# A four-layer graph network on one core: layer 3's first pair placed in layer 2, roots as powers on GpSimd, finer steps in the chains, and another split of the squares

## The chip, the cores and the metric

The kernel runs on one core of one Trainium2 chip. The metric is the device time of one execution in microseconds (us), over three runs of the kernel before. A core has a matrix engine (TensorE, PE; its weight loads are listed as PEld), a vector engine (VectorE, DVE), a scalar engine (ScalarE, ACT), a general engine (GpSimd, POOL) and an engine that here only issues transfers (SyncE, SP). Each engine works through its own instructions in their fixed order and waits on semaphores for the others.

## The reference, cut to what matters

`x` is 3327 x 64, `adj` is a dense 3327 x 3327 matrix with few nonzero values. Four layers follow each other; each takes a layer norm of `x` with a ReLU, a function of it and `adj`, and adds the result to `x`.

```python
h = maximum(layernorm(x), 0); x = x + ggc(ggc(h, adj), adj)  # layer 0, two gated steps
h = maximum(layernorm(x), 0); x = x + hyperbolic(h, adj)     # layer 1: adj @ h, norms, tanh, artanh
h = maximum(layernorm(x), 0); x = x + ranked(h, adj)         # layer 2:
#   mask = adj != 0; rank = cumsum(mask, 1); w = mask * 0.5 ** (k - pos); w @ (h @ weight) + bias
h = maximum(layernorm(x), 0)                                 # layer 3:
adj_att = sigmoid(left + right.T) * adj                      # per pair of nodes
x_local = logmap(h[:, None, :], h[None, :, :])               # per pair of nodes
s = einsum('ij,ijd->id', adj_att, x_local)
x = x + proj(expmap(h, s))                                   # per node: norms, tanh, quotients
```

## The kernel before

The nodes are padded to 26 blocks of 128 and stand on the free axis of the transposed matrix. They are cut into two target groups: group 0 with 12 blocks (1536 columns) and group 1, called `gf`, with 14 (1792 columns); `gs_` is group 0. A tile of `adj` is one source block by one target group: 768 or 896 KB. Every layer reads such tiles through one stream. `uses_of_tiles` (L125) lists all uses in order; `Stream` (L137) keeps tiles in numbered slots and, at each `done`, loads those up to 6 or 10 uses ahead that find a slot. `limit` (L155) says how many slots each layer has: 16 in layers 0 and 1, 7 in layer 2, 4 in layer 3. SP issues all loads, at L262.

Small chains of work for the nodes (norms, quotients, transposes) are Python generators. `Weave` (L81) advances each of them by one step at every `tick`, between the steps of the large loops, and a `yield 2` skips a tick. That is how the order on each engine comes about: what a generator issues before its next `yield` stands as one piece in the engines' queues.

Layer 1's result goes through `support` (L711), once per group, which also prepares layer 2's operands. `norm` (L443) and `layernorm_relu` (L450) take their square roots on ACT, followed by a reciprocal on DVE. ACT holds one set of function tables at a time; a root needs another set than Tanh or Gelu.

Layer 2 (L948 to L1046) goes over 52 tiles, 26 for group 1, then 26 for group 0. For tile n DVE makes the mask (L961) two tiles ahead, PE counts ranks with two triangular products per half (L975, L983) into a pair of PSUM banks, ACT turns counts to weights by a Relu (L991), and two tiles later PE multiplies the weights by three bfloat16 parts of the operands (L1009). After group 1's last tile its result is evicted, and `nodes3(gf)` (L819) makes what layer 3 needs of these nodes, in ticks between group 0's tiles: layer norm, `x2`, `q`, the scaled nodes `xd`, `pn` and its inverse `rpn`, transposed copies `xs` and `xw`, packed rows `rows_i`, `rows_j`, and `leftb`. `nodes3(gs_)` follows inside layer 3 and uses one PSUM bank, `turn["banks"] = (1,)`.

Layer 3 (L1140 to L1349) goes over 26 pairs of source blocks: 13 for the targets of group 1 and 13 for group 0; pairs 0 to 6 have sources in `gf`. For a pair, `distances(n, k)` runs PE (L1159, L1171), a Gelu over the result (L1179) and a Tanh (L1186) on ACT, for k = 0 and 1. `weights` (L1208) multiplies the Tanh by two adj tiles on DVE (L1214). `squares` (L1198) squares the Gelu's two halves: `a` on ACT (L1202), `b` in part on ACT (L1203) and the rest on DVE (L1204), cut by `split`. `products3` (L1217) multiplies both on DVE (L1223), and `gather` and `gather_p` (L1235, L1252) sum over sources on PE. The loop is skewed by two:

```python
for n in range(-2, len(pairs)):
    if n >= 0: products3(n); weave.tick()
    if 0 <= n + 1 < len(pairs): distances(n + 1, 1); weave.tick()
    if n >= 0: gather(n)
    if 0 <= n + 1 < len(pairs): weights(n + 1); weave.tick(); squares(n + 1); weave.tick()
    if n + 2 < len(pairs): begin(n + 2); distances(n + 2, 0); weave.tick()
    if n >= 0: gather_p(n)
    weave.tick()
```

After pair 12 group 1 is evicted, and `collected` with `finish` (L1053) computes its output in ticks beside pairs 13 and later; after pair 25 the same runs for group 0 with nothing beside it, and ends the kernel. A general branch after L1353 is for other inputs and is not taken.

Of the kernel before, what the change touches and what calls it, by code (L numbers as in the profile page):

```python
# [18 lines left out]
D = 64  # L19
# [24 lines left out]
SLOTS3, SLOTS2, SLOTS01 = 4, 7, 16  # L44
# [80 lines left out]
def uses_of_tiles():  # L125

    last_first = [2 * c + h for h in (1, 0) for c in reversed(range(HB))]
    layer2 = [(g, k) for g in (1, 0) for k in last_first]
    layer3 = [(g, k) for g in (1, 0) for k in F_SRC + S_SRC]
    starts, uses = [], []  # L130
    for u in (FIRST + SECOND + THIRD, LAYER1, layer2, layer3):
        starts.append(len(uses))
        uses += u
    return uses, starts[1:]


class Stream:  # L137
# [17 lines left out]
    def limit(self, t):  # L155
        layer = sum(t >= s for s in self.starts)
        return (SLOTS01, SLOTS01, SLOTS2, SLOTS3)[layer]

    def next_use(self, s, t):
# [4 lines left out]
        for u in range(t, len(self.uses)):  # L164
            if self.uses[u] == key:
                return u if s < self.limit(u) else len(self.uses)
        return len(self.uses)

    def ahead(self):
        most = AHEAD[self.now >= len(FIRST + SECOND)]  # L170
        for u in range(self.now, min(self.now + most, len(self.uses))):
            key = self.uses[u]
            if any(k == key and s < self.limit(u) for s, (k, _) in self.slots.items()):
                continue
            wanted = set(self.uses[self.now : u + 1])
            able = [
                s for s, (k, _) in self.slots.items() if s < self.limit(u) and k not in wanted
# [8 lines left out]
    def tile(self, u):  # L186
# [4 lines left out]
            if k == self.uses[u] and s < self.limit(u)  # L191
# [13 lines left out]
def gnn_kernel(ctx: ExitStack, tc: tile.TileContext, t, out):  # L205
# [13 lines left out]

    p0 = ctx.enter_context(left("p0"))  # L220
# [36 lines left out]
    def load_tile(s, key):  # L257
        g, k = key
        pool = slots_a if s < SLOTS3 else slots_b if s < SLOTS2 else slots_c
        a = pool.tile([P, WIDE], F32, name="adj", tag=f"adj{s}")  # L260
# [18 lines left out]
    V.memset(eps, LN_EPS)  # L279

# [162 lines left out]
    def norm(g, src, name):  # L443
        r = yield from sumsq(g, src, name)
        S.activation(r, r, AF.Sqrt)
# [4 lines left out]
    def layernorm_relu(g, dst):  # L450
# [8 lines left out]
        S.activation(var, var, AF.Sqrt, bias=eps, scale=1.0 / D)  # L459
        yield  # L460
        rstd = recip(g, var, "ln_rstd")
# [249 lines left out]
    def support(g, m_t):  # L711
# [5 lines left out]
        mn = yield from norm(g, mx, "n1")  # L717
# [28 lines left out]
        yield from layernorm_relu(g, h_n)  # L746
# [72 lines left out]
    def nodes3(g, m_t):  # L819
# [4 lines left out]
        yield from layernorm_relu(g, hv)  # L824
# [13 lines left out]
        S.activation(pn[:, sl], xv, AF.Sqrt)  # L838
# [12 lines left out]
        V.tensor_scalar(pn[:, sl], pn[:, sl], MIN_NORM, None, op0=OP.max)  # L851
        V.reciprocal(rpn[:, sl], pn[:, sl])
        V.tensor_mul(uq, uq, rpn[:, sl])
# [94 lines left out]
    with ExitStack() as c2:  # L948
        mk = c2.enter_context(right("l2"))
        WB = 7  # L950
        LAG = 2
        work = stream.uses[stream.starts[1] : stream.starts[2]]
# [3 lines left out]
        def mask(n):  # L956
            if n < len(work):
                a = stream.tile(stream.starts[1] + n)
                g = GROUPS[work[n][0]]
                masks[n] = mk.tile([P, WIDE], BF16, name="mask", tag="mask", bufs=4)  # L960
                V.tensor_scalar(masks[n][:, : 2 * g.w], a, 0.0, None, op0=OP.not_equal)  # L961

        def count(n, h):
# [3 lines left out]
            if h == 0:  # L967
                ws[n] = mk.tile([P, WIDE], U16, name="w", tag="w", bufs=WB)
# [62 lines left out]

        mask(0)
        mask(1)
        for n in range(len(work)):
            mask(n + 2)
# [4 lines left out]
            todo += [(n, 0), (n, 1)]  # L1040
            flush(n, 4 if len(todo) > 2 * LAG + 2 else 2)
            weave.tick()
        flush(len(work) + LAG, len(todo))
        m_s = evicted(gs_, acc2[0], b_l2)
        weave.until(need["nodes"])
# [7 lines left out]
    def finish(g):  # L1053
# [25 lines left out]
        yield  # L1079
        V.tensor_reduce(ss, w2, axis=AX.X, op=OP.add)  # L1080
        yield
# [4 lines left out]
        al = mul("f_al", fac, B)  # L1086
        be = small(g, "f_be")
        V.scalar_tensor_tensor(be, hs, 2.0, sd, op0=OP.mult, op1=OP.subtract)
        V.tensor_mul(be, be, fac)
        su = mul_add("f_su", al, ss, be, hs)  # L1090
        yield
        hu = mul_add("f_hu", al, hs, be, x2g)
# [4 lines left out]
        V.tensor_scalar(hl, Bp, MIN_NORM, None, op0=OP.max)  # L1097
        V.reciprocal(hl, hl)
        tau = mul("f_tau", pn[:, sl], hl)
        S.activation(tau, tau, AF.Tanh)  # L1100
# [5 lines left out]
        V.scalar_tensor_tensor(xy, hu, 2.0, tau, op0=OP.mult, op1=OP.mult)  # L1106
        V.tensor_scalar(xy, xy, 1.0, None, op0=OP.add)
# [3 lines left out]
        V.tensor_add(rden, rden, xy)  # L1111
# [511 lines left out]
```

## Time and profile before

| | us |
|---|---|
| three runs | 780.57, 780.72, 782.84 |
| median | 780.72 |
| profiled execution | 781.49 |
| its span, first to last instruction | 779.7 |
| PE busy | 670.8 |
| DVE busy | 452.7 |
| ACT busy | 419.2 |
| POOL busy | 4.8 |
| layers 0 and 1, until about | 308 |
| layer 2, until about | 469 |
| layer 3, until about | 751.6 (last gather starts) |
| last finish and output | to 779.7 |

Busy time counts an engine's instructions, not its waits. Matmuls are pipelined, so a full PE row is not PE at its peak. The span lies 1.8 us below the profiled execution's own time, and that execution 0.8 above the median. The mean granted TensorE clock was 0.958 of full speed. 229 tile loads took a median of 6.6 us (768 KB) and 7.5 us (896 KB) from issue to landing.

### The profile page before, as it was taken

What the parts mean: (1) busy time and instruction counts of PE and PEld (TensorE: products, weight loads), DVE (VectorE), ACT (ScalarE), POOL (GpSimd) and SP (SyncE); (2) the same over time, 40 slices, a digit from 0 to 9 for tenths busy, and PEclk for the clock granted to TensorE, in tenths of its full rate; (3) what the DMA queues carried; (4) which work ended last, traced back from release to release, by engine and by line L of the source; (5) the groups of instructions that cost most, each with busy time, mean ns of one, the idle gap of its engine ahead of it and who ended that gap; (6) DMA issues with size and microseconds to landing.
All of it is one profiled execution on the core that took longest, in us unless ns stands there. A gap on an engine that the chain in (4) does not pass through costs nothing. (4 is left out here: it accounts for less than half of the span.)

```text
span 779.7 us, 10293 instructions
## 1 busy us (share of the span) xinstructions
PE 670.8 (86%) x4141; PEld 292.3 (37%) x4141; DVE 452.7 (58%) x749; ACT 419.2 (54%) x489; POOL 4.8 (1%) x11
## 2 busy tenths in 40 slices
PE   4988998898879987799989995788999987799970
PEld 2423442343323333344445452333434433344430
DVE  4403002205776034853366425787999978999976
ACT  3203001203553023666666768777999966799941
POOL 0000000000000001000000000000000000000000
PEclk9999999999999999999999998699999998999995
DMA  8999893699949999989867842224555542265400
GB/s 348 413 407 418 325 366 157 212 391 417 415 176 421 417 414 417 417 323 340 279 224 243 298 152 95 95 95 156 192 191 205 172 165 82 104 211 193 164 1 24
DMA packets 34327, 197.56 MB, mean 253 GB/s; under 512 B 3808, under 2 KB 4448, under 8 KB 34272
## 3 DMA queue, kind: packets, MB, share of 16 engines
q1 hardware_dynamic: 34272, 196.84, 66.6%
q8 instruction: 34, 0.56, 0.3%
q14 instruction: 21, 0.17, 0.1%
HBM read 195.97 MB, written 0.85 MB: 252 GB/s over the span
## 5 line engine op out<-in xcount | busy, mean ns | idle before, releaser
L487 PE MATMUL bank<-adj,m_a 128*64 128x384 f32 (+1 forms) x832 | 159.5, 526 | 10.8 <-DMA adj<-in_adj 10.8
L991 ACT ACTIVATE w<-pair,ebias 128x896 uint16<-128x896 f32 (+1 forms) x104 | 94.4, 949 | 37.0 <-PE pair L983 36.5
L1159 PE MATMUL pair<-xw,xs 64*128 64x384 f32 x208 | 100.2, 563 | 12.9 <-ACT gl L1179 12.9
L1214 DVE SCALAR_TENSOR_TENSOR th<-th,adj 128x1792 f32<-128x1792 f32 (+1 forms) x52 | 97.7, 1891 | 5.8 <-ACT th L1186 5.2
L1159 PE MATMUL pair<-xs 64*128 64x384 f32 x208 | 100.2, 563 | 0.9 <-ACT gl L1179 0.9
L1223 DVE SCALAR_TENSOR_TENSOR gl<-gl,th 128x1792 f32<-128x1792 f32 (+5 forms) x78 | 97.5, 1306 | 0.4 <-issue 0.4
L1179 ACT ACTIVATE gl<-pair 128x896 f32<-128x896 f32 (+1 forms) x104 | 84.0, 862 | 24.8 <-PE pair L1171 24.7
L487 PEld LDWEIGHTS bank<-adj,m_a 128*64 128x64 f32 x832 | 56.6, 138 | 101.3 <-issue 69.8
L1235 PE MATMUL bank<-gl,xd 128*64 128x384 f32 (+1 forms) x416 | 85.2, 545 | 10.0 <-DVE gl L1223 8.8
L1186 ACT ACTIVATE th<-leftb,righth 128x1792 f32<-128x1792 f32 (+1 forms) x52 | 87.7, 1686 | 0.0
L961 DVE TENSOR_SCALAR mask<-adj 128x1792 bf16<-128x1792 f32 (+1 forms) x52 | 53.2, 1027 | 44.7 <-PE pair L975 42.5
L487 PE MATMUL bank<-adj,m_b 128*64 128x384 f32 (+1 forms) x416 | 78.1, 521 | 1.0 <-ACT hm L570 0.5
L975 PE MATMUL pair<-mask,rest 128*128 128x384 bf16 x200 | 68.1, 341 | 7.2 <-ACT w L991 7.2
L983 PE MATMUL pair<-mask,tri 128*128 128x384 bf16 x208 | 69.7, 339 | 1.4 <-DVE mask L961 1.4
L569 DVE COPY mh<-bank 64x384 f32<-64x384 f32 (+1 forms) x8 | 4.6, 581 | 100.7 <-PE bank L487 100.6
L570 ACT ACTIVATE hm<-bank 64x384 f32<-64x384 f32 (+1 forms) x8 | 4.1, 512 | 104.1 <-DVE mh L569 104.0
L1009 PE MATMUL bank<-w,m_b 128*64 128x384 bf16 (+1 forms) x416 | 54.9, 345 | 0.0
L1235 PEld LDWEIGHTS bank<-gl,xd 128*64 128x64 f32 x416 | 32.3, 143 | 57.6 <-issue 29.4
L1171 PE MATMUL pair<-rows_i,rows_j 64*128 64x384 bf16 x208 | 48.3, 347 | 0.0
L1159 PEld LDWEIGHTS pair<-xw,xs 64*128 64x128 f32 x208 | 35.5, 196 | 32.6 <-ACT gl L1179 29.5
L487 PEld LDWEIGHTS bank<-adj,m_b 128*64 128x64 f32 x416 | 28.7, 138 | 47.1 <-issue 42.1
L1159 PEld LDWEIGHTS pair<-xs 64*128 64x128 f32 x208 | 35.5, 196 | 27.4 <-issue 17.5
(271 smaller groups left out, 698.7 us busy)
## 6 DMA issues: line engine op xcount, KB each, us to landing
adj<-in_adj SPq DMA_DIRECT2D x110, 896.0 KB, 7.5
adj<-in_adj SPq DMA_DIRECT2D x119, 768.0 KB, 6.6
xn<-in_x SPq DMA_DIRECT2D x3, 192.0 KB, 4.9
w_l<-in_w_l SPq DMA_DIRECT2D x1, 460.0 KB, 10.0
out<-h_n SPq DMA_DIRECT2D x1, 448.0 KB, 4.0
out<-h_n SPq DMA_DIRECT2D x1, 384.0 KB, 2.7
xn<-in_x SPq DMA_DIRECT2D x1, 256.0 KB, 7.1
w_all<-in_w_all SPq DMA_DIRECT2D x1, 67.5 KB, 12.7
```

The source lines that it names most:

```text
L487: T.matmul(acc[q][h * D : (h + 1) * D, : hi - lo], lhsT=m[:, k, :], rhs=a[:, h * g.w + lo : h * g.w + hi], start=first, stop=last,)
L961: V.tensor_scalar(masks[n][:, : 2 * g.w], a, 0.0, None, op0=OP.not_equal)
L975: T.matmul(dst, lhsT=rest, rhs=masks[n - 1][:, cs], start=False, stop=False, skip_group_check=True,)
L983: T.matmul(dst, lhsT=tri, rhs=masks[n][:, cs], start=first, stop=True, skip_group_check=True,)
L991: S.activation(ws[n][:, h * g.w : (h + 1) * g.w], cnt[h][:, P : P + g.w], AF.Relu, bias=ebias, scale=-EXP_UNIT,)
L1009: T.matmul(acc2[i][q][h * D : (h + 1) * D, : hi - lo], lhsT=p[:, k, :], rhs=ws[n][:, h * g.w + lo : h * g.w + hi].bitcast(BF16), start=n % ...
L1159: T.matmul(pts[b][:, P + lo : P + hi], lhsT=xs[rs, c * P : (c + 1) * P], rhs=rhs[rs, g.c0 * P + lo : g.c0 * P + hi], start=True, stop=False,)
L1179: S.activation(gl[n][b][:, k * g.w : (k + 1) * g.w], pts[b][:, P : P + g.w], AF.Gelu, scale=-HA,)
L1186: S.activation(ths[n][k][:, : 2 * g.w], leftb[:, g.off : g.off + 2 * g.w], AF.Tanh, bias=righth[:, kk : kk + 1], scale=0.5,)
L1214: V.scalar_tensor_tensor(th, th, 1.0, a, op0=OP.add, op1=OP.mult)
L1223: V.scalar_tensor_tensor(a, a, hd, th[b][:, lo:hi], op0=OP.add, op1=OP.mult)
L1235: T.matmul(acc["x"][q][k * D : (k + 1) * D, : hi - lo], lhsT=xd[:, 2 * c + b, :], rhs=gl[n][b][:, k * g.w + lo : k * g.w + hi], start=firs ...
```

## The change

- Layer 3's pair 0 (distances, Gelu, Tanh, squares, weights, products) is issued inside layer 2, by a generator `first_pair` that runs behind `nodes3(gf)` and by DVE work at tiles 46 and 47. Its two adj tiles enter the stream at that place. Layer 3's loop then begins with pair 1, and pair 0 has only its gathers left.
- Room for this: layer 2 keeps 5 slots plus two further ones (16 and 17) until tile 30, and after group 1 three instead of seven weight buffers. Pair 0's buffers are a pool of their own.
- In layer 2's second half there are three ticks per tile instead of two, and the wait for `nodes3(gf)` at the layer's end is gone.
- Square roots in `support`, both `nodes3` and the first `finish` become a power of -0.5 on POOL, with one Newton step on DVE two ticks later. The last `finish` keeps its root on ACT.
- `finish` yields more often.
- `split`: pairs 1 to 6 give ACT 1024 instead of 512 columns of `b`; pairs 14 to 19 give it all of `b`.

```diff
-SLOTS3, SLOTS2, SLOTS01 = 4, 7, 16
+SLOTS3, SLOTS2, SLOTS01, MORE2 = 4, 5, 16, (16, 17)
+LESS2 = NB + 5
+EARLY3 = 2 * NB - 6
...
+    layer2[EARLY3:EARLY3] = layer3[:2]
+    del layer3[:2]
...
+    def valid(self, s, t):
+        if s in MORE2:
+            return self.starts[1] <= t <= self.starts[1] + LESS2
         layer = sum(t >= s for s in self.starts)
-        return (SLOTS01, SLOTS01, SLOTS2, SLOTS3)[layer]
+        return s < (SLOTS01, SLOTS01, SLOTS2, SLOTS3)[layer]
...
+    minus_half = p0.tile([P, GROUPS[1].nb], F32, name="minus_half")
+    V.memset(minus_half, -0.5)
...
+    def inverse_root(g, r, v):
+        G.tensor_tensor(r, v, minus_half[:, : g.nb], op=OP.pow)
+        yield 2
+        e = small(g, "inv_e")
+        V.tensor_mul(e, r, r)
+        V.scalar_tensor_tensor(e, e, -0.5, v, op0=OP.mult, op1=OP.mult)
+        V.scalar_tensor_tensor(r, e, 1.5, r, op0=OP.add, op1=OP.mult)
...
+        if power:
+            V.tensor_scalar(var, var, 1.0 / D, LN_EPS, op0=OP.mult, op1=OP.add)
+            rstd = small(g, "ln_rstd")
+            yield from inverse_root(g, rstd, var)
+        else:
+            S.activation(var, var, AF.Sqrt, bias=eps, scale=1.0 / D)
+            yield
+            rstd = recip(g, var, "ln_rstd")
...
-        S.activation(pn[:, sl], xv, AF.Sqrt)
+        pv, rp = pn[:, sl], rpn[:, sl]
+        V.tensor_scalar(pv, xv, MIN_NORM**2, None, op0=OP.max)
+        yield
+        yield from inverse_root(g, rp, pv)
+        V.tensor_mul(pv, pv, rp)
+        V.tensor_mul(uq, uq, rp)
...
-        WB = 7
+        WB, WL = 7, 3
...
+        def first_pair():
+            c, g = gf.c0, gf
+            for k in range(2):
+                for lo, hi in g.chunks:
+                    pts = [bank(2 + b)[:, : hi - lo] for b in range(2)]
...
+                    for b in range(2):
+                        S.activation(
+                            gl[0][b][:, k * g.w + lo : k * g.w + hi], pts[b], AF.Gelu, scale=-HA
+                        )
+                    yield 2
+                kk = 2 * c + k
+                S.activation(ths[0][k], leftb[:, g.off : g.off + 2 * g.w], AF.Tanh,
+                    bias=righth[:, kk : kk + 1], scale=0.5)
+                yield 2
+            a, b = gl[0]
+            V.scalar_tensor_tensor(b, b, 2 * HG, b, op0=OP.add, op1=OP.mult)
+            S.activation(a, a, AF.Square, bias=hg)
+            yield
...
         for n in range(len(work)):
+            if n == LESS2 - 1:
+                stream.close(MORE2)
...
+                gen_e = weave.add(first_pair(), 1, need["nodes"])
+            if n == EARLY3:
+                weave.until(gen_e)
+                for th in ths[0]:
+                    a = stream.tile(stream.now)
+                    V.scalar_tensor_tensor(th, th, 1.0, a, op0=OP.add, op1=OP.mult)
+                    stream.done()
             mask(n + 2)
...
+            if n >= NB:
+                weave.tick()
             flush(n, 4 if len(todo) > 2 * LAG + 2 else 2)
+            if n == EARLY3 + 1:
+                for b, hd in enumerate((HD, HD + HG * HG)):
+                    a = gl[0][b]
+                    V.scalar_tensor_tensor(a, a, hd, ths[0][b], op0=OP.add, op1=OP.mult)
             weave.tick()
...
-        weave.until(need["nodes"])
...
+        if loop:
+            ni = small(g, "f_ni")
+            yield from inverse_root(g, ni, nn)
+        else:
+            S.activation(nn, nn, AF.Sqrt)
...
-        def split(g):
-            return g.w // 2 + 64, 2 * g.w
+        def split(n):
+            g = GROUPS[pairs[n][0]]
+            if HB < n <= HB + 6:
+                return 2 * g.w, 2 * g.w
+            return g.w // 2 + (576 if n < 7 else 64), 2 * g.w
...
-        for n in range(-2, len(pairs)):
+        for n in range(-1, len(pairs)):
...
-            if n >= 0:
+            if n == 0:
+                gather(n)
+            if n > 0:
                 products3(n)
                 weave.tick()
                 if n == HB:
-                    final = weave.add(collected(gf, *evict(gf)))
+                    final = weave.add(collected(gf, *evict(gf), True))
-            if 0 <= n + 1 < len(pairs):
+            if 0 < n + 1 < len(pairs):
                 distances(n + 1, 1)
                 weave.tick()
-            if n >= 0:
+            if n > 0:
                 gather(n)
-            if 0 <= n + 1 < len(pairs):
+            if 0 < n + 1 < len(pairs):
                 weights(n + 1)
```

## The prediction

> **What bounds the kernel now.** I cut the trace by stage first (the table of stretches), since the page's shares average over stages with different limits.
>
> ```profile
> 308.00:396.00 88.00, 80.71 (x562) 38.67 (x564) 46.00 (x64) 60.22 (x71) 0.00 (x0) 1.00 0.91 340
> 396.00:469.00 73.00, 69.50 (x574) 37.66 (x570) 37.03 (x69) 49.16 (x62) 0.00 (x0) 1.00 0.63 219
> 469.00:538.20 69.20, 49.83 (x270) 22.16 (x268) 50.78 (x69) 53.12 (x53) 0.00 (x0) 0.85 0.30 107
> 538.20:633.30 95.10, 93.64 (x564) 38.96 (x562) 92.97 (x66) 88.93 (x81) 0.00 (x0) 1.00 0.53 185
> 633.30:686.50 53.20, 40.11 (x237) 18.50 (x237) 45.91 (x78) 35.83 (x39) 0.00 (x0) 0.87 0.36 123
> 686.50:751.60 65.10, 61.69 (x427) 28.52 (x426) 63.78 (x48) 59.91 (x61) 0.00 (x0) 1.00 0.44 151
> ```
>
> Columns: stretch, length, busy time of PE, weight loads, DVE, ACT, POOL, then granted clock, DMA share, GB/s. Rows one and two are layer 2: its second half is PE's (69.5 of 73), ACT has 24 us free. Rows four and six are layer 3 in its rhythm, with PE, DVE and ACT all near full, so nothing is won there. Rows three and five are the holes: the filling of layer 3's pipeline (no engine above 77%) and the time just after pair 12, when the first half of the result is finished beside pairs 13 to 16. PE starts its gathers (L1235) like this in the timeline:
>
> ```profile
> 496.73 4.42 PE L1235 MATMUL bank<-gl,xd 128*64 128x384 f32 x16
> 508.96 3.64 PE L1235 MATMUL bank<-gl,xd 128*64 128x384 f32 x16
> 523.68 3.26 PE L1235 MATMUL bank<-gl,xd 128*64 128x384 f32 x16
> 538.22 3.23 PE L1235 MATMUL bank<-gl,xd 128*64 128x384 f32 x16
> ```
>
> Layer 2's last matmul starts at 468.7, so the first gather comes 27.8 us into layer 3, and the next three are 12.2, 14.7 and 14.5 us apart where the rhythm is 9.35. ACT's timeline shows the cause inside the filling:
>
> ```profile
> 478.33 0.84 ACT L437 ACTIVATE sq<-xc 128x768 f32<-128x768 f32 x1
> 479.19 1.28 ACT L459 ACT_TABLE_LOAD   x1
> 481.39 0.30 ACT L459 ACTIVATE ln_var<-ln_var,eps 128x12 f32<-128x12 f32 x1 [0.92 <-DVE ln_var L440]
> 484.01 1.28 ACT L1179 ACT_TABLE_LOAD   x1
> 489.45 1.28 ACT L838 ACT_TABLE_LOAD   x1
> 490.98 1.28 ACT L1179 ACT_TABLE_LOAD   x1
> ```
>
> Two square roots of the node chain cost four table loads between Gelus. In the second hole:
>
> ```profile
> 658.28 0.21 ACT L1100 ACTIVATE f_tau<-f_tau 128x14 f32<-128x14 f32 x1 [6.34 <-DVE f_tau L1063]
> 661.38 1.28 ACT L1121 ACT_TABLE_LOAD   x1
> 662.90 1.28 ACT L1179 ACT_TABLE_LOAD   x1
> ```
>
> ACT sat 6.34 us until a tiny Tanh at the end of a DVE chain was ready, with the next Gelu queued behind it; then a root takes two more loads.
>
> **What the Trainium skill says.** ScalarE: Activation LUTs, "What ACT_TABLE_LOAD costs": about 1283 ns for a load and 1380 ns of drain. The trace agrees on 1.28; it shows no separate drain (489.45 to the root at 490.75 is 1.30), so I price a switch at 1.3. Same page, "Table sets": cheap functions such as relu and copy are in every set, costly ones anchor their own. Here Square and Relu follow any set without a load, and Tanh follows Gelu without one. GPSIMD Engine Reference, "Elementwise — side-by-side cycle accounting": about 2.6 cycles an element with two inputs. No page prices a power, and POOL ran none here. TensorE: Matmul & The Clock Gate, Part 1: a PE idle for some 3.4 us falls to half clock; the trace agrees, with granted clocks of 0.61 and 0.54 in the slices at 480 and 490.
>
> **The change, part by part.** Durations are before's. I laid them by hand into the changed kernel's instruction order (which I read per engine), each operation after its engine's last and after its inputs. t is time since layer 2's last matmuls.
>
> *First pair out of the filling.* At t=0 only pair 1 has to be made. ACT: Gelu and Tanh for k=0 end at 5.6 (2.1 of distances, 1.6, 1.7). PE runs the transposes of m_t and gather(0), 3.2 us, to 6.4, then distances (1,1) to 8.5; Gelu and Tanh end at 11.9, a square for the nodes and the pair's two at 15.4. DVE: second weights 11.9 to 13.9, variance 14.9, its square 16.0, root and h 18.6, products to 22.6; gather(1) starts half-way, at 20.6, against 40.0 before. Between products(1) and products(2) DVE has 2.5 (x, q, xd) + 3.9 (weights) + 0.9 + 1.4 (eight small ones) + 4.0 = 12.7. The transposes of xd share one bank whose copy (xs) sits behind products(2), so gather(2) starts at 37.8. Continued likewise, with the round trips of rows_i, rows_j and leftb through that bank: 47.9, 60.5, 70.8, 81.3 for gathers 3 to 6. Before, gather(6) started at 566.87, t=97.9. Gain 16.6, four table loads included.
>
> *The same pair beside layer 2.* PE pays the distances, 2 x 2.1 = 4.2, where it is full. ACT gets, in the stretch from the Gelu load to the first pair's square: one load 1.3, eight Gelu pieces 4.1, two Tanh 3.4, a square 1.7, and eight of layer 2's relus, 6.7: 17.2. PE has there four tiles at 2.5 and the distances, 14.2. ACT is normally 0.8 to 1.2 ahead per tile, so PE waits some 2.0 more. Cost 6.2; bounds 4.2 (PE alone) and 10 (no slack usable). DVE adds b's square 2.0, weights 3.9 and products 4.0 over ten tiles in which it has 1.5 free each: hidden, as masks are issued two tiles ahead. The removed wait for the nodes at layer 2's end was already met.
>
> *Denser node chain in layer 2 (three ticks a tile).* PE lost 3.5 us at 396 to 420 to relus late behind the chain's squares; the same work in fewer tiles: 1.0 more (0 to 3).
>
> *Layer 1 to 2.* In the support of layer 1's result two loads go (318.6, 329.7), worth up to 2.5; four extra ticks delay the second group's operands by about two tiles, so that PE has less to weigh at tile 9 and 10: 1 to 2. I take 0 (-2 to 2). Five instead of seven slots prefetched: the two missing loads are issued after the first tile's release instead of four steps earlier. SP's queue then still has tiles 2 to 4 to deliver, 2.2 us each, so DMA never idles: 0. With five slots in the second half a load is released five tiles before its mask, 12 us, and lands within 6.6 (median): 0; total loads stay 229.
>
> *Squares.* Pairs 1 to 6 move 512 columns from DVE (0.55) to ACT (0.45): in the sum above. Pairs 14 to 19 give ACT all of b's square: DVE loses 1.2 a pair, ACT gains 1.0 and goes to 9.3, above the 8.2 rhythm.
>
> *Finish in small steps, power for its root.* DVE between products: 13 to 14 10.5 plus two waits, 14 to 15 12.2, 15 to 16 9.8, 16 to 17 13.2. gather(17) starts 48.7 us after gather(13), against 53.2; before this the gain is larger (9 at pair 16), the tail of four 896-wide operations, now in a row, takes some back. Then ACT at 9.3 holds pairs 18 to 20: about 1 us is lost again. Gain 4 (1 to 8).
>
> *End.* The last finish keeps its root on ACT, runs nothing beside it, and has the same operations: 0.
>
> *The powers.* Nine on POOL. Bounds: below, a few fixed costs (its 128x1 iota took 0.13); above, open. Each value is used two ticks later, behind a mask (0.95) or b's short square (0.9), twice behind products or weights (over 3.4). I take 1 us, all hidden.
>
> Sum against the profiled execution, 781.5 (span 779.7): -16.6 + 6.2 + 1.0 + 0 - 4 = -13.4, hence 768.1. The median shown is 0.8 lower, so 767.
>
> **Rivals.**
> 1. ScalarE becomes the bound. Tail costs 10, the moved squares stand on the path (6 x 0.45 = 2.7), the finish gives nothing, the nodes cost 2: 780.7 - 16.6 + 10 + 2.7 + 2 = 779. For it: ACT is at 93% in the rhythm. Against: ACT waits 7.1 us on PE in the filling and 11 in the second hole.
> 2. More is won: PE keeps its clock in both holes (0.85 and 0.87 now), and denser work lifts the gains to 22 and 8 with 4.2 paid: 755.
> 3. Slower: the power is long. DVE takes the result in order, so what POOL needs beyond its cover stops masks, weights and products. Seven powers lie in layers 2 and 3, with covers 1.1, 1.1, 0.95, 0.95, 0.9, 4.8 and 3.4. The excess eats 13.4 at about 3.7 us each if nothing absorbs it, at some 7 if the masks' lead does. At 10 us the excess is 57, less 16 of lead: 780.7 - 13.4 + 41 = 808. For it: nothing in the trace bounds it. Against: 128 lanes work on only 12 or 14 values each.
> 4. The change doesn't do what it says: the instruction order shows the pair ahead of layer 2's last ten tiles and the eight loads gone, so only a pair finished late (PE waiting at its gather) is left; within rival 1.
>
> **How the numbers follow.** Forecast 0.66 (own range 760 to 775), rival 1 0.12, rival 2 0.07, rival 3 0.15. Within 0.3% (2.3 us) of 780.7 is what a measurement can't tell from no change. Rival 1 lies half in that band. Faster 0.66 + 0.07 + 0.06 = 0.79; same 0.06; slower 0.15. The range 754 to 780 leaves out rival 3 and the edges of 1 and 2, about 0.2.
>
> **What would show it.** Right: gather(1) some 21 us after layer 2's end and gather(6) at 81; no table load between layer 2's Gelu load and the last root; layer 2's second half 7 us longer; gather(17) 49 us after gather(13). Wrong: DVE idle before the root's correction with POOL as releaser; ACT at 100% and PE waiting for relus over more than five tiles; gathers 14 to 20 at 9.3 or more throughout; a DMA named as releaser of masks after tile 28.

## The result, and the profile after

The changed kernel takes 786.47 us (median of 4 executions, 785.13 to 788.30), the kernel before 781.41 beside it (780.57 to 782.84): a ratio of 1.0064, with a 95% interval of 1.0038 to 1.0091. It is slower by about 5 us; the forecast was 767. The profiled execution has a span of 784.8 us, against 779.7 before.

First the table of stretches of the changed kernel, cut at the same events in both kernels: the evictions of m_t at the end of layer 1, in the middle and at the end of layer 2, then gathers 6, 13 and 20 of layer 3. The columns are those of the prediction's table (stretch, length, busy time of PE, weight loads, DVE, ACT and POOL, granted clock, DMA share, GB/s).

```profile
306.08:403.31 97.23, 87.04 (x573) 41.80 (x571) 49.68 (x74) 58.38 (x69) 6.74 (x3) 0.95 0.81 302
403.31:487.59 84.28, 76.47 (x592) 40.05 (x590) 47.25 (x80) 58.19 (x72) 6.39 (x2) 0.96 0.64 228
487.59:573.42 85.83, 72.55 (x420) 29.43 (x416) 66.59 (x89) 66.75 (x63) 6.88 (x2) 0.94 0.37 130
573.42:639.72 66.30, 65.09 (x393) 27.26 (x392) 65.99 (x46) 61.91 (x57) 0.00 (x0) 1.00 0.53 182
639.72:716.13 76.41, 65.92 (x403) 28.06 (x403) 62.63 (x86) 62.05 (x60) 4.03 (x1) 0.91 0.44 151
716.13:784.80 68.67, 43.01 (x298) 19.72 (x297) 56.09 (x85) 39.43 (x42) 0.00 (x0) 0.86 0.22 77
```

| stretch | before | after | difference | predicted |
|---|---|---|---|---|
| A: layer 1's eviction to layer 2's first | 89.8 | 97.2 | +7.4 | 0 |
| B: to layer 2's second eviction | 72.5 | 84.3 | +11.8 | +7.2 |
| C: to gather(6) | 98.3 | 85.8 | -12.4 | -16.6 |
| D: gather(6) to the end | 212.8 | 211.4 | -1.5 | -4 |

In A seven transposes have moved behind the cut. Cut one eviction earlier, A holds the same 692 matmuls in both kernels. It stands here before and after, then B before:

```profile
279.30:396.14 116.84, 104.41 (x692) 46.99 (x690) 60.27 (x94) 69.06 (x83) 3.85 (x3) 1.00 0.94 359
279.59:403.31 123.72, 109.16 (x692) 49.34 (x690) 62.43 (x107) 63.51 (x76) 15.07 (x7) 0.96 0.86 326
396.14:468.60 72.46, 68.96 (x568) 37.53 (x566) 36.63 (x69) 49.02 (x62) 0.00 (x0) 1.00 0.63 220
```

So A's loss is 6.9 us for the same work. In 4.8 of them PE is busy longer, in 2.1 it is idle longer. The granted clock, 1.00 before, is 0.50 for some 3.4 us from 314.8, from 338.6 and from 352.3 on, so most of the loss shows as slower matmuls. No run parts this loss of clock from the waits that came with it. In B PE is busy 7.5 us longer, part of it with the pair's own work, and the clock is 0.96 in place of 1.00.

C is shorter, as intended. D is the sum of the last three rows. What happens up to the first eviction differs between executions (it came at 304.5 to 307.9 us in the profiles of this study), so I compare stretches, and medians. A stretch is read from one execution. Two kernels below that are the same from layer 3 on differ by 1.0 us in D, so less than that says nothing there.

The gathers of layer 3's filling, in PE's timeline of the changed kernel (start, duration, instruction):

```profile
510.30 3.72 PE L1366 MATMUL bank<-gl,xd 128*64 128x384 f32 x16 [0.76 <-DVE gl L1354]
526.85 4.67 PE L1366 MATMUL bank<-gl,xd 128*64 128x384 f32 x16
538.91 3.23 PE L1366 MATMUL bank<-gl,xd 128*64 128x384 f32 x16
552.60 3.23 PE L1366 MATMUL bank<-gl,xd 128*64 128x384 f32 x16
563.47 3.23 PE L1366 MATMUL bank<-gl,xd 128*64 128x384 f32 x16
573.42 3.57 PE L1366 MATMUL bank<-gl,xd 128*64 128x384 f32 x16
```

They come 22.3, 38.9, 50.9, 64.6, 75.5 and 85.4 us after layer 2's last matmuls (their end, 488.0; before, 469.0). The prediction had 20.6, 37.8, 47.9, 60.5, 70.8 and 81.3. In ACT's timeline the only table load left in or after layer 2, up to the last root, is the one ahead of the first pair's Gelus; and the small Tanh of the finish waits 1.29 us where it waited 6.34 and holds no load behind it:

```profile
444.26 1.28 ACT L1103 ACT_TABLE_LOAD   x1
...
663.42 0.21 ACT L1210 ACTIVATE f_tau<-f_tau 128x14 f32<-128x14 f32 x1 [1.29 <-DVE f_tau L1171]
```

So the change does what it says. What is new is in POOL's groups (busy us, then mean ns of one):

```profile
L459 POOL TENSOR_TENSOR ln_rstd<-ln_var,minus_half 128x14 f32<-128x14 f32 (+1 forms) x4 | 11.8, 2941 | 174.5 <-DVE ln_var L489 174.5
L459 POOL TENSOR_TENSOR rpn<-pn,minus_half 128x14 f32<-128x14 f32 (+1 forms) x2 | 7.1, 3572 | 14.1 <-DVE pn L873 8.0 <-PE pair L1027 6.0
L459 POOL TENSOR_TENSOR inv<-n,minus_half 128x14 f32<-128x14 f32 (+1 forms) x2 | 5.6, 2822 | 300.2 <-DVE n L469 300.2
L459 POOL TENSOR_TENSOR f_ni<-f_nn,minus_half 128x14 f32<-128x14 f32 x1 | 4.0, 4030 | 154.5 <-DVE f_nn L1232 154.5
```

A power takes 2.8 to 4.0 us on average, where I assumed 1. DVE's waits on it between 308 and 490 us, from the list of waits (us in total, times, longest):

```profile
DVE inv_e L462 <- POOL ln_rstd L459: 4.6, 2, 2.5
DVE inv_e L462 <- POOL rpn L459: 2.5, 1, 2.5
DVE inv_e L462 <- POOL inv L459: 2.2, 1, 2.2
```

And one such wait in the timeline, in layer 2's second half:

```profile
411.43 0.96 DVE L1003 TENSOR_SCALAR mask<-adj 128x1536 bf16<-128x1536 f32 x1
411.61 3.23 POOL L459 TENSOR_TENSOR ln_rstd<-ln_var,minus_half 128x14 f32<-128x14 f32 x1 [71.02 <-DVE ln_var L489]
414.87 0.17 DVE L462 TENSOR_TENSOR inv_e<-ln_rstd 128x14 f32<-128x14 f32 x1 [2.48 <-POOL ln_rstd L459]
...
416.62 0.25 DVE L861 TENSOR_SCALAR h<-h,lastf 128x64 f32<-128x64 f32 x1
416.97 0.95 ACT L863 ACTIVATE sq<-h 128x896 f32<-128x896 f32 x1 [5.19 <-DVE h L861]
417.82 0.88 ACT L1035 ACTIVATE w<-pair,ebias 128x768 uint16<-128x768 f32 x1
```

One mask of 0.96 us is all the cover there is, that is, work of DVE between a power's issue and the use of its value. DVE then stands 2.48 us. ACT's square needs h, so ACT stands 5.19 us, and the relu (w) that PE waits for is queued behind that square. PE's waits on w in layer 2's second half, before and after (us in total, times, longest):

```profile
PE pair L975 <- ACT w L991: 2.5, 4, 0.8
PE pair L1019 <- ACT w L1035: 7.4, 4, 5.0
```

### The profile page after: what moved, and what is told of

Read it like the earlier page. It is cut to its first block, busy times and chain, and to the rows that moved or that the text cites. A ratio compares the mean times of both kernels' runs of the same rounds, so it can differ in the third digit from the quotient of the medians.

```text
span 784.8 us, 10303 instructions
## 1 busy us (share of the span) xinstructions
PE 677.1 (86%) x4141; PEld 290.2 (37%) x4141; DVE 446.6 (57%) x765; ACT 412.2 (53%) x474; POOL 33.4 (4%) x20
## 5 line engine op out<-in xcount | busy, mean ns | idle before, releaser
L1344 DVE SCALAR_TENSOR_TENSOR th<-th,adj 128x1536 f32<-128x1536 f32 (+1 forms) x50 | 93.7, 1885 | 16.5 <-ACT th L1311 16.2
L1366 PE MATMUL bank<-gl,xd 128*64 128x384 f32 (+1 forms) x416 | 86.1, 550 | 12.4 <-DVE gl L1354 11.2
L1284 PE MATMUL pair<-xw,xs 64*128 64x384 f32 x200 | 93.1, 546 | 3.1 <-ACT gl L1304 3.0
L1304 ACT ACTIVATE gl<-pair 128x768 f32<-128x768 f32 (+1 forms) x100 | 80.6, 860 | 28.1 <-PE pair L1296 27.6
L1284 PE MATMUL pair<-xs 64*128 64x384 f32 x200 | 93.7, 549 | 1.0 <-ACT gl L1304 1.0
L521 PEld LDWEIGHTS bank<-adj,m_a 128*64 128x64 f32 x832 | 56.6, 138 | 102.3 <-issue 68.7
L1354 DVE SCALAR_TENSOR_TENSOR gl<-gl,th 128x1536 f32<-128x1536 f32 (+7 forms) x69 | 93.5, 1408 | 0.5 <-ACT f_tau L1210 0.5
L1311 ACT ACTIVATE th<-leftb,righth 128x1536 f32<-128x1536 f32 (+1 forms) x50 | 84.1, 1682 | 0.0
L1019 PE MATMUL pair<-mask,rest 128*128 128x384 bf16 x200 | 69.7, 349 | 11.8 <-ACT w L1035 11.8
L1027 PE MATMUL pair<-mask,tri 128*128 128x384 bf16 x208 | 71.4, 347 | 2.0 <-DVE mask L1003 2.0
L1053 PE MATMUL bank<-w,m_b 128*64 128x384 bf16 (+1 forms) x416 | 57.8, 360 | 1.1 <-DVE m_b L798 1.1
L1296 PE MATMUL pair<-rows_i,rows_j 64*128 64x384 bf16 x200 | 44.6, 341 | 0.0
L1383 PE MATMUL bank<-gl,p2c 128*32 128x384 f32 (+1 forms) x416 | 44.5, 519 | 0.0
L1284 PEld LDWEIGHTS pair<-xs 64*128 64x128 f32 x200 | 33.1, 191 | 26.2 <-issue 16.5
```

Of the source, the lines that this page charges most:

```text
L521: T.matmul(acc[q][h * D : (h + 1) * D, : hi - lo], lhsT=m[:, k, :], rhs=a[:, h * g.w + lo : h * g.w + hi], start=first, stop=last,)
L1019: T.matmul(dst, lhsT=rest, rhs=masks[n - 1][:, cs], start=False, stop=False, skip_group_check=True,)
L1027: T.matmul(dst, lhsT=tri, rhs=masks[n][:, cs], start=first, stop=True, skip_group_check=True,)
L1053: T.matmul(acc2[i][q][h * D : (h + 1) * D, : hi - lo], lhsT=p[:, k, :], rhs=ws[n][:, h * g.w + lo : h * g.w + hi].bitcast(BF16), start=n % ...
L1284: T.matmul(pts[b][:, P + lo : P + hi], lhsT=xs[rs, c * P : (c + 1) * P], rhs=rhs[rs, g.c0 * P + lo : g.c0 * P + hi], start=True, stop=False,)
L1304: S.activation(gl[n][b][:, k * g.w : (k + 1) * g.w], pts[b][:, P : P + g.w], AF.Gelu, scale=-HA,)
```

## The experiments

Theory A: the powers' length stops DVE, which takes its work in order, and ACT and PE behind it. Theory B: the denser chain and the first pair's load on ACT beside layer 2 cost the time, and DVE's waits lie beside other waits. Every time below is a median, and every ratio is against executions of the kernel before on the same chip (its medians there were 780.95 to 781.86).

**Only the power's length (`short_op`).** The roots' values are left out.

```diff
-        G.tensor_tensor(r, v, minus_half[:, : g.nb], op=OP.pow)
+        G.tensor_tensor(r, v, minus_half[:, : g.nb], op=OP.subtract)
...
-        V.scalar_tensor_tensor(e, e, -0.5, v, op0=OP.mult, op1=OP.mult)
+        V.scalar_tensor_tensor(e, e, 0.0, v, op0=OP.mult, op1=OP.mult)
```

> The changed kernel with a subtraction in the place of each of the nine powers on POOL (and a factor of 0 in the correction, so that values stay finite): every instruction stays on its engine, in its order and with its waits, only POOL's operation is shorter; the roots' values are left out, so the output is not the reference's. Theory A (the length of the power: DVE, in order, stands 2 to 2.7 us per power, 12.2 us in all from layer 1's end on, and ACT and PE behind it): DVE's waits on POOL fall under 1 us each and the time falls from 786.5 by 9 to 13, to 773 to 777. Theory B (the denser chain, the third tick and the first pair's load on ACT beside layer 2 cost it; DVE's waits are hidden by other waits): 784 to 787. About 780 would give both half.

Measured: 777.41 us, ratio 0.9939 (0.9912 to 0.9966). With the same instructions, order and waits, a shorter operation on POOL is worth 9.1 us (786.47 - 777.41). A falls from 97.2 to 93.3, B from 84.3 to 80.8, D from 211.4 to 210.4, and C stays at 86.3: in the filling the long powers cost nothing that can be seen. PE's wait of 5.0 us on w is 2.7 here. Theory A holds, 0.4 us above its range. But A is still 3.5 us above before, though DVE no longer waits for POOL there. Cut one eviction earlier it is 3.0, of which PE is busy longer in 2.7 (107.1 for 104.4), at a clock of 0.97.

**All roots back on ACT (`roots_act`).**

```diff
-        mn = yield from norm(g, mx, "n1", power=True)
+        mn = yield from norm(g, mx, "n1")
...
-                    final = weave.add(collected(gf, *evict(gf), True))
+                    final = weave.add(collected(gf, *evict(gf), False))
```

(and likewise in the two layernorms and for pn)

> The changed kernel with all nine roots back on ACT as a square root, and all else of the change kept (first pair, ticks, squares, small steps of finish). Theory A: the waits on POOL go, about 2.5 us for two table loads in front of layer 2 and two to four loads in the filling come back: 776 to 780, below before's 781.4. Theory B: the time stays or rises by the loads: 786 to 791.

Measured: 781.03 us, 0.9988 (0.9974 to 1.0003): no difference from before that can be told, 5.4 better than the changed kernel, 1.0 above what A expected. The parts say why. A is 89.8, B 80.6, C 93.7, D 209.5. So the first pair costs B 8.1 us; and with the four table loads back in the filling (at 491.97, 497.21, 502.65 and 504.18) C gains 4.5 instead of 12.4. The powers at layer 3's start are therefore worth 7.9 us; those in layer 2 cost A 7.4 and B 3.7.

**The powers without the rest (`before_pow`).**

```diff
-        S.activation(var, var, AF.Sqrt, bias=eps, scale=1.0 / D)
-        yield
-        rstd = recip(g, var, "ln_rstd")
+        V.tensor_scalar(var, var, 1.0 / D, LN_EPS, op0=OP.mult, op1=OP.add)
+        rstd = small(g, "ln_rstd")
+        yield from inverse_root(g, rstd, var)
```

(in the kernel before, and likewise for the other roots)

> The kernel before with the nine powers alone (same correction on DVE, same yield of two ticks), nothing else of the change. Theory A: 12 us of waits on POOL come, some 5 us of table loads go: 786 to 791, slower than 781.4. Theory B: the powers are harmless and the loads gone: 776 to 781.

Measured: 784.27 us, 1.0041 (1.0018 to 1.0064). Slower, by less than A said: A 95.6 (+5.8), B 74.1 (+1.7), C 94.2 (-4.1), D 214.3 (+1.4). The sign is A's, the size is not: A and B lose 5.8 and 1.7 here, and 7.4 and 3.7 with the rest of the change beside the powers.

**Without the third tick (`no_tick`).**

```diff
-            if n >= NB:
-                weave.tick()
```

> The changed kernel without the third tick per tile in layer 2's second half (two ticks a tile as before). Theory A: within 1.5 us of the changed kernel, 785 to 788. Theory B (the chain's squares and copies crowd the relus on ACT, so PE waits for them): 778 to 783.

Measured: 787.61 us, 1.0082 (1.0060 to 1.0104); B 84.25 against 84.28. Beside the long powers the denser chain is free, and this half of theory B falls. What B holds beside the powers is the pair with what it brings along (its slots and buffers were not tried apart).

**Powers only at layer 3's start (`gs_powers`)**, and the same with other squares (`gs_powers_split`) or a slower pair (`gs_powers_spread`).

```diff
-        yield from layernorm_relu(g, hv, power=True)
+        yield from layernorm_relu(g, hv, power=g is gs_)
```

(pn likewise; the powers of `support` and of the finish off)

> The changed kernel with powers only where a Gelu would be split by table loads (the two of the second group's node chain, at layer 3's start); the five around layer 2 and the one of finish back on ACT. Theory A (a power costs where PE is full and DVE's order is tight; it pays where it removes loads between Gelus): to the eviction in layer 2 as before, 89.8 us; layer 2's second half 80.6 as with all roots on ACT; layer 2's end to gather(6) 85.8 as in the changed kernel; from gather(6) to the end 209.5; sum 773 to 775. Theory B (the run-to-run differences hide the parts, they do not add): 777 to 781.

Measured: 775.37 us, 0.9933 (0.9913 to 0.9953). The parts add as written down, but for D (209.5 was expected): A 89.8, B 80.6, C 85.8, D 210.6. The median lies 0.4 above its range.

```diff
-            if HB < n <= HB + 6:
-                return 2 * g.w, 2 * g.w
-            return g.w // 2 + (576 if n < 7 else 64), 2 * g.w
+            return g.w // 2 + 64, 2 * g.w
```

> The same with the squares split as in the kernel before (64 columns past the half for every pair). If the moved squares make ACT late in the filling (gathers 3 to 6 came 1 to 4.7 us later than the prediction laid them): the way from layer 2's end to gather(6) falls from 85.8 to 82 or 83. If they help there as they were counted: it rises by 3 (6 pairs by 0.5). In the rest, pairs 14 to 19: within 1.5 us either way.

Measured: 780.35 us, 0.9978 (0.9964 to 0.9992), 5.0 slower. C rises to 88.4 and D to 212.8: beside the first pair, moving squares to ACT helps in both places, in D by more than the 1.5 us that I had allowed. They are not what makes the gathers late.

```diff
-EARLY3 = 2 * NB - 6
+EARLY3 = 2 * NB - 3
...
-                    yield 2
+                    yield 3
```

> As gs_powers, with the first pair spread over more of layer 2 (three ticks between its pieces in the place of two, its last work due three tiles later). If the pair's cost beside layer 2 (8.1 us with roots on ACT) is ACT's crowding over four to six tiles: layer 2's second half falls from 80.6 to 77 or 78. If it is PE's own added work and the lost prefetch: it stays at 80 to 81.

Measured: 774.14 us, 0.9911 (0.9894 to 0.9928). B fell only to 79.65, less than either reading said, so 0.9 of the 8.1 us was crowding. C rose by 0.9 in exchange. From layer 3 on this kernel is gs_powers; D is 209.6 against 210.6.

**The other way round: the kernel before, plus parts.** The first has the powers at layer 3's start and the new finish (`before_gs_fin`).

```diff
+        pv, rp = pn[:, sl], rpn[:, sl]
+        if g is gs_:
+            V.tensor_scalar(pv, xv, MIN_NORM**2, None, op0=OP.max)
+            yield
+            yield from inverse_root(g, rp, pv)
```

(the layernorm likewise, and the changed finish with its root on ACT)

> The kernel before with the two powers at layer 3's start and finish in small steps (root on ACT), without the first pair, the ticks, the split and the slots. If the first pair is worth what the parts say (costs 8.1 beside layer 2, saves 12.4 less the 4.1 that go with the loads alone): equal to gs_powers within 1.5 us, 773 to 776. If the pair pays beyond the loads: 777 to 780.

Measured: 778.47 us, 0.9967 (0.9955 to 0.9980). That is in the range for a pair that pays beyond the loads, but it doesn't decide, since this kernel lacks the split, too. C is 95.6 and D 214.8, two above before (1.2 of them after gather(20)), so small steps alone show no gain.

The split alone (`before_split`) is before with the changed `split`, `squares` and `products3`:

```diff
-            return g.w // 2 + 64, 2 * g.w
+            if HB < n <= HB + 6:
+                return 2 * g.w, 2 * g.w
+            return g.w // 2 + (576 if n < 7 else 64), 2 * g.w
```

> The kernel before with the changed split of the squares alone (more of them on ACT in pairs 0 to 6 and 14 to 19). gs_powers against gs_powers_split put 5.0 us on the split, with the first pair and the powers beside it. If it is worth that by itself: 776 to 778. If it only pays once the table loads and the first Gelus are out of the filling: 780 to 784, since in the filling ACT is the late engine.

Measured: 782.37 us, 1.0014 (0.9996 to 1.0033). By itself it does nothing (C 99.3, D 212.6).

The next one (`before_gs_split`) has that split and the two powers at layer 3's start, both shown above, and the finish as before:

> The kernel before with the split and the two powers at layer 3's start; finish as before, no first pair, no ticks, no slots. If the first pair costs beside layer 2 what it saves later (8.1 against 7.2 plus 2.0 by the parts): 773 to 776, the same as gs_powers at 775.4. If the first pair is worth something that the split needs: 777 to 780.

Measured: 775.30 us, 0.9902 (0.9875 to 0.9929), the same as gs_powers with its 775.37. Without the first pair B is 72.5 and C 94.5; with it 80.6 and 85.8. The pair costs 8.1 and saves 8.6.

**More cover (`cover`), and the finish.**

```diff
         G.tensor_tensor(r, v, minus_half[:, : g.nb], op=OP.pow)
-        yield 2
+        yield 4
```

> The changed kernel with four ticks in the place of two between each power and its correction. If what the powers cost is DVE standing in order behind them (theory A): DVE's waits on POOL go and the time falls from 786.5 to 778 to 782. If it is the longer chain (more ticks until the nodes' operands are there, so PE runs out of work that it may do): it stays or rises, 785 to 790.

Measured: 780.06 us, 0.9976 (0.9961 to 0.9990), 6.4 better than the changed kernel. This agrees with A in the sum but not in place: DVE still waited 4.6 us on POOL in layer 2, A went down 1.9 and B 2.0, and D from 211.4 to 207.7.

In the next run (`gs_powers_old_finish`) `finish` is, as a whole, that of the kernel before, in gs_powers:

```diff
         V.tensor_reduce(hs, w1, axis=AX.X, op=OP.add)
+        yield
+        V.tensor_reduce(ss, w2, axis=AX.X, op=OP.add)
+        yield
```

> gs_powers with finish in the coarse steps of the kernel before. The prediction counted 4 us (1 to 8) for the small steps. If they give that: 778 to 781. If what is won after gather(13) comes from the squares on ACT and not from the steps, as before_gs_fin's 214.8 from gather(6) to the end against before's 212.8 suggests: within 1.5 us of 775.4.

Measured: 775.75 us, 0.9920 (0.9894 to 0.9946): a tie, with D at 213.0 against 210.6. With the root on ACT the small steps are worth some 2 us at most. Against before_gs_split this kernel adds the pair alone, with its ticks, slots and buffers: 775.75 and 775.30, with A and D equal to 0.1 us. That is the cleanest sign that the pair is worth nothing here.

Two questions stood open: what of A is left with a short operation (`short_op_one_tick`), and whether the 71.4 us that `cover` took from gather(13) to gather(20) are real.

```diff
         G.tensor_tensor(r, v, minus_half[:, : g.nb], op=OP.subtract)
-        yield 2
+        yield
```

> short_op (a subtraction in the place of each power, the roots' values left out) with one tick instead of two between it and its use, as the root on ACT had. If the later chain is what is left of the powers' cost in layer 2's first half: from the eviction in layer 1 to the one in layer 2 falls from 93.3 to 90 or 91, and the time from 777.4 to about 774. If it is the four added instructions on DVE for each root: 93 and 777.

Measured: 778.61 us, 0.9966 (0.9953 to 0.9979), where 774 was expected. A fell to 90.1 as the later chain said; the added instructions on DVE cost next to nothing there. But B rose from 80.8 to 84.0 and the time did not fall. A chain that starts earlier meets other tiles in the next half; why that costs 3 us I have not found.

```diff
-            yield from inverse_root(g, ni, nn)
+            yield from inverse_root(g, ni, nn, 4)
...
-                    final = weave.add(collected(gf, *evict(gf), False))
+                    final = weave.add(collected(gf, *evict(gf), True))
```

(`best_pair`, in gs_powers_spread; the last argument of `inverse_root` is the number of ticks to the root's use)

> gs_powers_spread with finish's root as a power again, but used four ticks later. If the finish's gain is real once its power is covered: gather(13) to gather(20) 71 to 73 against 74.5, and 770 to 772.5 against 774.1. If not: 774 to 776.

Measured: 772.17 us, 0.9884 (0.9864 to 0.9903); gather(13) to gather(20) took 71.1.

The last one (`best_no_pair`) is before_gs_split with the changed finish and that same covered power:

```diff
-                    final = weave.add(collected(gf, *evict(gf)))
+                    final = weave.add(collected(gf, *evict(gf), True))
```

> The kernel before with three parts only: the two powers at layer 3's start, the changed split, and finish in small steps with a power used four ticks later. No first pair, ticks or slots. If the finish's gain holds without the pair: gather(13) to gather(20) 71 to 73 against 77.9 in before_gs_split, and 769 to 772. If it needs the pair: 775.

Measured: 771.09 us (767.63 to 773.42), 0.9871 (0.9846 to 0.9897). It beats both kernels, by some 10 us the one before and by 15 the changed one, and ties with best_pair. Its table of stretches up to gather(20), with the cuts of the first table:

```profile
305.03:394.84 89.81, 81.24 (x566) 38.71 (x564) 47.65 (x68) 60.87 (x72) 0.00 (x0) 1.00 0.91 341
394.84:467.30 72.46, 68.95 (x568) 37.53 (x566) 36.60 (x69) 49.02 (x62) 0.00 (x0) 1.00 0.62 221
467.30:561.73 94.43, 80.29 (x445) 33.53 (x441) 74.87 (x95) 77.23 (x72) 6.84 (x2) 0.93 0.38 137
561.73:628.10 66.37, 65.23 (x393) 27.37 (x392) 66.05 (x46) 61.84 (x57) 0.00 (x0) 1.00 0.51 182
628.10:699.50 71.40, 63.46 (x403) 26.89 (x403) 62.43 (x87) 62.08 (x59) 4.03 (x1) 0.95 0.47 161
```

Layer 2 is before's, to a tenth of a microsecond. What changed is the filling (94.4 for 98.3) and the stretch after gather(13) (71.4 for 77.8); the last stretch is 1.3 longer (69.9 for 68.6). POOL is busy 4.03 us with that power, exactly as in the changed kernel, so the 5.0 us between the two (76.4 and 71.4) are not POOL's. DVE's timeline shows them. First the changed kernel, then this one:

```profile
677.29 0.17 DVE L462 TENSOR_TENSOR inv_e<-f_ni 128x14 f32<-128x14 f32 x1 [0.79 <-POOL f_ni L459]
...
678.84 3.42 DVE L1344 SCALAR_TENSOR_TENSOR th<-th,adj 128x1536 f32<-128x1536 f32 x2
682.18 1.08 DVE L1249 TENSOR_TENSOR h_n<-sums,f_ka 128x896 f32<-128x896 f32 x1
683.18 1.08 DVE L1251 TENSOR_TENSOR xc<-h,f_ch 128x896 f32<-128x896 f32 x1
684.18 1.08 DVE L1253 TENSOR_TENSOR h_n<-h_n,xn 128x896 f32<-128x896 f32 x1
685.30 1.09 DVE L1255 TENSOR_TENSOR h_n<-h_n,xc 128x896 f32<-128x896 f32 x1
686.31 3.42 DVE L1354 SCALAR_TENSOR_TENSOR gl<-gl,th 128x1536 f32<-128x1536 f32 x2
```

```profile
666.81 1.76 DVE L1262 SCALAR_TENSOR_TENSOR th<-th,adj 128x1536 f32<-128x1536 f32 x1 [0.21 <-ACT th L1229]
668.49 0.17 DVE L450 TENSOR_TENSOR inv_e<-f_ni 128x14 f32<-128x14 f32 x1
...
670.07 1.09 DVE L1173 TENSOR_TENSOR h_n<-sums,f_ka 128x896 f32<-128x896 f32 x1
671.08 1.08 DVE L1175 TENSOR_TENSOR xc<-h,f_ch 128x896 f32<-128x896 f32 x1
```

In the changed kernel all four wide operations of the finish stand in one row between a pair's weights and its products, 4.2 us for which the next gather waits. With the root used two ticks later only two of them stand there. DVE's wait for POOL itself was only 0.79 us. That gather is gather(17), first in the changed kernel, then the first half of it in this one:

```profile
688.12 5.39 PE L1366 MATMUL bank<-gl,xd 128*64 128x384 f32 x16 [3.55 <-DVE gl L1354]
```

```profile
673.88 1.51 PE L1284 MATMUL bank<-gl,xd 128*64 128x384 f32 x8 [0.85 <-DVE gl L1272]
```

It comes 48.4 and 45.7 us after gather(13), which is 2.7 of the 5.0 us. The other 2.3 follow: the changed kernel's clock is 0.50 from 686.8 to 693.6, so that this gather alone takes 5.39 us, while the other kernel's clock is 1.00 from 672 to 682. `cover`, which differs from the changed kernel in the ticks alone, agrees (71.4).

## Why the prediction was wrong

**The step that failed is "The powers": "I take 1 us, all hidden".** They took 2.6 to 4.0 us, and for each of the four in layer 2 DVE stood 2.2 to 2.5 us beyond its mask. Their length is worth 9.1 us (short_op). Against roots on ACT the powers with their ticks cost 7.4 in A (6.9 by the earlier cut) and 3.7 in B: 11.1 of the 18.5 us between the predicted -13.4 and the measured +5.1 of the span. Rival 3 had this mechanism and this sign: the excess over the cover stops DVE. Its price of about 3.7 us a power, if nothing absorbs it, was near. I gave it 0.15 because 12 or 14 values a lane seemed little work. With no price for a power anywhere, that was no argument. The length alone did not turn the sign, though. With short operations the kernel takes 777.4, faster than before and still 10 above the forecast of 767; the terms below are the rest.

There was a second error beside that step: what the root on ACT cost where it stood. In layer 2 ACT runs Relu, which needs no load after a root (the Trainium skill, ScalarE: Activation LUTs, "Table sets": cheap functions are in every set; the trace agrees, as the stretch from 330 us to the Gelu load at 430 of gs_powers, with its two roots, shows no other load). The powers there removed two loads, at 318 and 329 us, which I had counted at up to 2.5 us. They were hidden: A is 89.8 with roots on ACT and their loads, before's number, and no better, 90.1, without them and with short operations (short_op_one_tick). At layer 3's start a root splits Gelus, and the two powers save 7.9 us with the pair and 4 to 5 without it.

**First pair out of the filling, -16.6: measured -12.4.** Right in kind, too large by 4.2. gather(1) was 1.7 late against my layout and gather(6) 4.1. The length of the powers is not the cause (86.3 with the short operation), nor are the moved squares (88.4 without them). What else holds gathers 3 to 6 back was not tried.

**The pair beside layer 2, +6.2, and the denser chain, +1.0: measured +8.1 together**, with the tick at nothing. Inside the bounds of 4.2 to 10. (Of the 3.5 us said to be lost to relus at 396 to 420, 2.5 were such waits.) I did not ask what the pair nets without the four loads: 8.1 against 8.6, a wash, and with the loads in place it gains only 4.5 for its 8.1 (roots_act). Much of what I credited to it in the filling belongs to the powers.

**Layer 1 to 2, 0 (-2 to 2): measured +3.5** with the powers' length taken out (A of short_op, 93.3 against 89.8; 3.0 by the earlier cut), outside its range. Its "four extra ticks, 1 to 2 us" were real: two of them, in front of the second group's operands, cost about 3 us (93.3 to 90.1; 2.5 by the earlier cut), and the hidden loads set nothing off against it. The 0 for fewer slots holds: roots_act has them, and A is 89.8.

**Finish, -4: measured -1.5 in D**, and -2.2 to -3.4 with the root on ACT (gs_powers, roots_act). The layout was right up to gather(17), which starts 48.4 us after gather(13), laid at 48.7. The term that failed is "about 1 us is lost again": from there to gather(20) the changed kernel takes 28.0 us, the one before 24.6. Of these 3.4, 0.9 lies between gathers 18 and 19, where ACT's work for a pair takes 9.1, about as laid. The other 2.5 lies between gathers 17 and 18, where PE works at half the clock after its wait of 3.55 us and ACT stands 5.08 us for PE. The prediction named the four wide operations in a row, but put nothing on the clock. With the row split D is 5.1 below before (best_no_pair).

**End, 0, and stream:** as predicted. The last stretch is 68.7 against 68.6, and the only wait for a DMA seen in layer 2's second half was 0.45 us. Rival 1 (ACT the bound) falls: in A to C ACT is busy at most 78% of a stretch, and moving squares back to DVE made it slower.

## What to carry to other kernels

Moving a small operation to another engine pays by what it takes off the path where it stands, so price it place by place: here a root cost nothing that could be seen on ACT between Relus, and two of them some 4 to 8 us between Gelus. An operation without a price must not be taken at the size of its data; if its result is read by an in-order engine, the cover ahead of the read has to exceed the worst price, and where the following work lands matters as much as the wait. And when two parts of a change act on the same stretch, ask what each is worth without the other before adding them up.

## What the runs showed of the hardware

A power of 128x14 values on POOL took 2.60 us with DVE idle, 3.2 beside a mask and 4.03 beside products. The subtraction in its place shows how it grows with the DVE instruction that is running. POOL and DVE in short_op, three places from the timeline:

```profile
296.86 0.22 POOL L459 TENSOR_TENSOR ln_rstd<-ln_var,minus_half 128x14 f32<-128x14 f32 x1 [11.40 <-DVE ln_var L489]
...
406.40 0.96 DVE L1003 TENSOR_SCALAR mask<-adj 128x1536 bf16<-128x1536 f32 x1
406.58 0.86 POOL L459 TENSOR_TENSOR ln_rstd<-ln_var,minus_half 128x14 f32<-128x14 f32 x1 [71.15 <-DVE ln_var L489]
...
503.98 3.96 DVE L1344 SCALAR_TENSOR_TENSOR th<-th,adj 128x1792 f32<-128x1792 f32 x2
504.15 1.92 POOL L459 TENSOR_TENSOR rpn<-pn,minus_half 128x12 f32<-128x12 f32 x1 [8.04 <-DVE pn L873]
```

The subtraction takes 0.22 us alone. Beside a mask it ends 0.08 us after the mask (407.44 and 407.36), beside the weights 0.11 after the first of the two (each 1.98). SBUF — State Buffer of the Trainium skill, "Who interferes with whom", says that a VectorE instruction with two SBUF inputs contends with a GpSimd instruction that reads SBUF, and that the one that issues first holds the port pair that they share for the whole instruction. The weights agree. The mask has one SBUF input, which that page lets contend only in a 2-port mode; the trace doesn't name its mode, but shows that it goes through 1792 values in 1.09 us where the weights take 1.98. The consequence here is that DVE work laid over a POOL operation as cover lengthens it first: with a mask of 0.96 us ahead of the read DVE waited 2.48 us for the power, with nothing ahead of it 2.70 (at 302.97 in the changed kernel). Work that DVE begins after that does cover: the power at 514.74, behind two weights and a short square, cost no wait.

A wait of PE does not by itself tell whether its clock falls. The stretches at half the clock in A of the changed kernel follow waits of 2.0, 2.5 and 1.8 us, shorter than the 3.4 us that the prediction went by; in the kernel before a wait of 2.4 us near 310 was followed by none, and in gs_powers and gs_powers_split, which are the same up to there, the same wait was followed by none and by one. A is 89.8 and 90.1 there. What decides whether the clock falls, and what a fall costs elsewhere, is not shown here.
